# A selective scan with softplus of two pieces side by side, a diagonal product on TensorE and another order of products and scans

## The chip, the core and the metric

The kernel runs on one core of a Trainium2 chip. The metric is the device time of one execution in microseconds (us). Engines are named TensorE (PE in the profile; PEld is its weight load), VectorE (DVE), ScalarE (ACT), GpSimd (POOL) and SyncE (SP, which here only issues DMAs).

## The reference, cut to what matters

The reference has two layers on `x` of shape (8, 64, 64, 96): a convolution with a four-way selective scan, then attention without softmax and a quantized feed-forward part. Only the scan is touched by the change:

```python
# B = 8, L = 4096, D_INNER = 192, D_STATE = 16, DT_RANK = 6, K = 4 directions
x_dbl = jnp.einsum('bkdl,kcd->bkcl', xs, x_proj_weight)
dts, Bs, Cs = x_dbl[:, :, :6], x_dbl[:, :, 6:22], x_dbl[:, :, 22:]
dts = jnp.einsum('bkrl,kdr->bkdl', dts, dt_projs_weight)
delta = jax.nn.softplus(dts + dt_projs_bias[None, :, :, None])
A = -jnp.exp(A_logs).reshape(K, D_INNER, D_STATE)
def step(h, inps):                     # along L, one h for each channel and state
    d_t, u_t, b_t, c_t = inps
    h = h * jnp.exp(d_t[..., None] * A) + (d_t * u_t)[..., None] * b_t[:, :, None, :]
    y = jnp.einsum('bkdn,bkn->bkd', h, c_t)
    return (h, y)
# then y + D * u, and the sum over the four directions
```

## The kernel before, in words

`pass1` makes the normalized input, its projections, the convolution with SiLU (`u`), and the projections to dt, B and C, all to HBM scratch. `pass2` is the scan. `pass3` does everything from the layer norm on. The change lies in `pass2` and in the class `Slots`.

**Tiling of the scan.** `pass2` works on 192 pieces. A piece (index `at`) is 128 channel rows by T = 1024 positions. The 192 channels of a pair of batches are cut into three chunks: c = 0 and c = 1 are 128 channels of one batch each, c = 2 holds the remaining 64 channels of both batches (so a "half" in what follows is one batch's 64 rows of it). For each of 4 pairs, 3 chunks and 4 directions `k` there are 4 pieces in a row, with directions 2 and 3 running backwards. 128 pieces have c < 2, 64 have c = 2.

**What one piece does.** `prepare` loads `xdt` (the split parts of dt), `xb` (the parts of B) and `u`; TensorE makes `bT` (B with positions on partitions) and the product of `xdt` and `dt_w`; ScalarE makes `delta` from that by softplus; GpSimd makes `du` = delta * u; TensorE transposes it and ScalarE copies it out as `duT`. Then for each of 16 states n:

- `decay`: ScalarE makes `da` = exp(delta * A_n), in one of three buffers.
- the input of the scan, `dbu` = du * B_n in a PSUM buffer `wide` (three of them), in one of three ways. By ScalarE (`scaled`): eight multiplications of `duT` blocks with a column of `bT`, sixteen halves where c = 2, giving `x`, and eight transposes on TensorE. By GpSimd (`scaled_by_pool`): the same in one multiplication (two where c = 2), giving `xg`. Otherwise TensorE spreads B_n over the partitions with two bf16 matmuls, and VectorE multiplies that by `du` in place. `WAYS` lists, for c < 2 and for c = 2, the states of the first and of the second way; those left over take the third, which this document calls products on VectorE.
- `scan`: VectorE's tensor_tensor_scan of `da` and `dbu` into half of an `h` tile (two states in one, three tiles). `carries` has ScalarE copy the last column, for the next piece of the same direction.
- `times_c`: for every two states GpSimd multiplies `h` by C, loaded broadcast over partitions by SP (`load_c`, six buffers `c`).
- `sum_over_n`: TensorE transposes these products into the accumulator `acc` and so sums over n. For k = 0 the sum begins with `ud` = u times the sum of D over the directions, made by ScalarE and transposed; for k >= 2 it begins with the earlier direction's `ys`. `take_acc` copies `acc` to `y`.

**What sets the order.** Every engine is wrapped in `InOrder`: its instructions run in the order in which the program issues them. That order comes from `weave`, a planner that runs while the kernel is built. Each unit of work is a generator that yields (engine, cost in us, delay before its result is usable, optional buffer slots) or a key that it waits for. `weave` always takes the step that can begin first by its own clock and, among equals, that of lower rank. The rank is `at * N + n - lead`, and the lead is the number given in `add`. A second table says how many units of a kind can be open at once. `Slots` plans when a buffer comes free.

Of the kernel before, what the change touches and what calls it, by code (L numbers as in the profile page):

```python
# [54 lines left out]
WAYS = [([2, 5, 6, 8, 11, 12, 14, 15], [3, 7]), ([2, 3, 7, 9, 14], [0, 5, 12])]  # L55
NS = 3

# [70 lines left out]
class Slots:  # L128


    def __init__(self, count):
        self.count, self.taken, self.ends = count, 0, {}

    def when(self):

        return 0.0 if self.taken < self.count else self.ends.get(self.taken + 1 - self.count)
# [405 lines left out]
def pass2(ctx, tc, g, ident, engines, fixed, u_d, xd_d, b_d, dt_d, y_d):  # L542
# [7 lines left out]
    room = {"c": 6, "da": 3, "h": 3, "x": 3, "wide": 3, "xg": 1, "ud": 1, "acc": 1}  # L550
# [8 lines left out]
    done, counts, made, ys, carry = {}, {}, {}, {}, {}  # L559
# [13 lines left out]
    def prepare(at):  # L573
# [10 lines left out]
        yield "sp", 2.5, 3.0  # L584
        xdt = one.tile([2 * NS * NS * R, T], BF16, name="xdt")
        queue = sp if at else pool
        for j in range(2):
            for m in range(NS):
                row = (j * NS + m) * NS * R
                queue.dma_start(xdt[row : row + NS * R, :], dt_d[2 * pair + j][o][k2].rearrange("s r t -> (s r) t")[:, cols])  # L590
        if at > 0:
            yield "sp", 1.5, 3.0
# [18 lines left out]
        yield "pe", 0.9, 0.2, slots["wide"]  # L611
        pd, slot = take("wide", [P, T])
        for q in range(0, T, GRP):
            pe.matmul(pd[:, q : q + GRP], dt_w[:, c, k, :], xdt[:, q : q + GRP], start=True, stop=True)

        end = yield "act", 3.6, 0.2
        delta = two.tile([P, T], F32, name="delta")
        act.activation(delta, pd, AF.Softplus, bias=dt_b[:, c // 2, k : k + 1])
        slots["wide"].release(slot, end)
        made[at] = [xb, u, delta, None, None, bT]  # L620
        done["delta", at] = end
        end = yield "pool", 2.37, 0.2
        du = two.tile([P, T], F32, name="du")
        pool.tensor_mul(du, delta, u)
        made[at][3] = du
# [6 lines left out]
        made[at][4] = two.tile([P, NT, P], F32, name="duT")  # L632
        act.copy(made[at][4], pt)
        slots["wide"].release(slot, end)
        done["duT", at] = end

# [18 lines left out]
    def decay(at, n):  # L655

        _, c, k, _ = pieces[at]
        yield "delta", at
        end = yield "act", 1.06, 0.2, slots["da"]
        da, slot = take("da", [P, T])  # L660
        act.activation(da, made[at][2], AF.Exp, scale=a_neg[:, c // 2, k, n : n + 1])
        made["da", at, n] = da, slot
        done["da", at, n] = end

    def scaled(at, n):

        pair, c, _, _ = pieces[at]
        yield "duT", at
        x, (_, _, _, _, duT, bT) = None, made[at]
        for i in range(0, NT, 2):  # L670
            cost = 0.6 if c < 2 else 1.0
            end = yield ("act", cost, 0.2) if i else ("act", cost, 0.2, slots["x"])
            if i == 0:
                x, slot = take("x", [P, NT, P])
            for i2 in (i, i + 1):
                for j, (part, _, _) in enumerate(chunk_rows(pair, c)):
                    act.mul(x[:, i2, part], duT[:, i2, part], bT[:, i2, j * N + n : j * N + n + 1])
        made["x", at, n] = x, "x", slot
        done["x", at, n] = end

    def scaled_by_pool(at, n):
# [4 lines left out]
        _, _, _, _, duT, bT = made[at]  # L686
# [7 lines left out]
    def products(at, n):  # L694
# [3 lines left out]
        if n in by_act or n in by_pool:  # L698
            yield "x", at, n
            end = yield "pe", 1.3, 0.2, slots["wide"]  # L700
# [5 lines left out]
        else:  # L706
# [6 lines left out]
            end = yield "dve", 1.22, 0.0  # L713
            dve.tensor_mul(dbu, made[at][3], dbu)
# [3 lines left out]
    def scan(at, n):  # L718
# [6 lines left out]
        if n % 2 == 0:  # L725
            end = yield "dve", 2.26, 0.2, slots["h"]
            made["h", at, n // 2] = take("h", [P, 2, T])
            done["begun", at, n // 2] = 0.0
        else:
            yield "begun", at, n // 2  # L730
            end = yield "dve", 2.26, 0.2
# [39 lines left out]
    def sum_over_n(at, m):  # L771
# [10 lines left out]
        if m == 0 and k == 0:  # L782
            yield "delta", at
            yield "act", 1.05, 0.2, slots["ud"]
            ud, slot = take("ud", [P, T])
            act.mul(ud, made[at][1], dsum[:, c // 2 : c // 2 + 1])
            end = yield "pe", 1.2, 0.0, slots["acc"]
            made["acc"] = take("acc", [P, NT, P])
            add(ud, True, False)
            slots["ud"].release(slot, end)  # L790
# [10 lines left out]
        for i in range(2):  # L801
            if m == 0 and k == 1 and i == 0:
                end = yield "pe", 1.2, 0.0, slots["acc"]
                made["acc"] = take("acc", [P, NT, P])
            else:
                end = yield "pe", 1.2, 0.0
# [32 lines left out]
    for at, (pair, c, k, pc) in enumerate(pieces):  # L839
# [5 lines left out]
        add("prep", 8, prepare(at))  # L845
        for n in range(N):
            if n % 2 == 0:
                add("c", 12, load_c(at, n // 2), n)
            add("da", 2, decay(at, n), n)
# [6 lines left out]
            if n % 2 == 1:  # L856
                if at % NPC < NPC - 1:
                    add("carry", -2, carries(at, n // 2), n)
                add("term", 0, times_c(at, n // 2), n)
                add("sum", -4, sum_over_n(at, n // 2), n)  # L860
        add("acc", 0, take_acc(at), N)
    last = [(b, o, w) for b in range(LATE, NB) for o in range(2) for w in splits(b, o, b_d, dt_d)]
    units += [("split", 5 * N * (i + 1), late_split(*which)) for i, which in enumerate(last)]
    weave(units, {"prep": 1, "c": 1, "da": 2, "x": 1, "xg": 1, "dbu": 2, "scan": 2, "carry": 1, "term": 1, "sum": 1, "acc": 1, "split": 1}, done)
# [300 lines left out]
```

## Time and profile before

| What | Value |
| --- | --- |
| Time, median of 3 runs (lowest to highest) | 10121.8 us (10119.1 to 10127.6) |
| Span of the profiled execution | 10130.1 us |
| Scan pass in it: first scan begins, last ends | 719 us, 9328 us |
| Busy share of the span: VectorE, ScalarE, GpSimd, TensorE | 94%, 91%, 89%, 74% |
| Scans on VectorE with / without a carried value | 2304 of 2332 ns, 768 of 2271 ns |
| Products on VectorE (`wide<-du,wide`) | 1280 of 1208 ns |
| Exponentials on ScalarE (`da`) | 3072 of 1144 ns |
| `x` on ScalarE: whole blocks, halves | 8192 of 390 ns, 5120 of 335 ns |
| Table loads on ScalarE | 386 of 1283 ns |
| `c` times `h` on GpSimd | 1536 of 4557 ns |

The profile lists instructions by group: engine, operation, the tile written and the tiles read, count, busy time and mean duration, and after the bar the time in which the engine stood idle just before such an instruction, with what released it. Most instructions carry the line of the helper that records them (L91), so groups are told apart by tiles. Successive instructions of one engine overlap a little: the end of one lies behind the start of the next. What an instruction costs in a full queue is therefore its distance from start to start, which the timeline shows, and not its duration.

### The profile page before, as it was taken

How to read it: one execution, taken by the hardware profiler on the slowest of the kernel's cores; microseconds unless marked ns; L12 is line 12 of the kernel's file. 1: busy time of each engine (PE TensorE's matmuls, PEld its weight loads, DVE VectorE, ACT ScalarE, POOL GpSimd, SP SyncE). 2: the span in 40 equal slices, each digit the busy share in tenths (PEclk: the TensorE clock that was granted, in tenths of full speed). 3: DMA queues.
4: the chain of work that ended last, by engine and by line, in shares of the span. 5: the costliest groups of instructions: out<-in, count | busy, mean ns of one | idle time of the engine just before them, and what ended most of it. 6: DMA issues, size and time to landing. Idle time of an engine off the chain costs nothing.

```text
span 10130.1 us, 152413 instructions
## 1 busy us (share of the span) xinstructions
PE 7527.0 (74%) x52384; PEld 6235.5 (62%) x52384; DVE 9551.4 (94%) x7025; ACT 9186.9 (91%) x20692; POOL 8990.2 (89%) x2911
## 2 busy tenths in 40 slices
PE   7767777777777777777777777777777777776777
PEld 3336666665666666666666666655666666565666
DVE  7869999999999999999999999999999999998887
ACT  5669999999999999999999999999999999997776
POOL 1439999999999999999999999999999999998665
PEclk8889998989998989989999989999989999998887
DMA  5766776789976776799966766899767667998652
GB/s 167 233 205 215 225 236 217 229 210 206 209 219 213 225 218 214 223 211 200 223 211 214 230 212 223 212 205 209 217 213 225 218 212 224 208 203 183 192 151 77
DMA packets 932228, 2111.66 MB, mean 208 GB/s; under 512 B 274603, under 2 KB 422860, under 8 KB 929922
## 3 DMA queue, kind: packets, MB, share of 16 engines
q1 hardware_dynamic: 928650, 2100.57, 74.0%
q8 instruction: 419, 6.86, 0.3%
q14 instruction: 351, 2.88, 0.1%
q0 software_dynamic: 432, 0.94, 0.0%
q10 hardware_dynamic: 2376, 0.40, 0.0%
HBM read 1925.98 MB, written 175.66 MB: 207 GB/s over the span
## 4 chain that ended last, share of the span: by engine, by line
DVE 30%; ACT 29%; issue 15%; PE 13%; POOL 9%; DMA 3%; SPq 1%; DVEq 0%; ACTq 0%; POOLq 0%
DVE h L91 20%; ACT x L91 11%; ACT da L91 10%; POOL c L91 7%; PE acc L91 6%; DVE wide L91 5%; PE wide L91 3%; ACT L91 2%; ACT y L91 1%; POOL xg L91 1%; PE px L91 1%; PE pa L91 1%; ACT delta L91 1%; DMA xd_d<-xd 1%; DVE u L91 1%
## 5 line engine op out<-in xcount | busy, mean ns | idle before, releaser
L91 POOL TENSOR_TENSOR c<-c,h 128x2048 f32<-128x2048 f32 x1536 | 6959.5, 4557 | 300.0 <-issue 139.4
L91 DVE TENSOR_TENSOR_SCAN h<-da,carry,wide 128x1024 f32<-128x1024 f32 x2304 | 5268.3, 2332 | 137.5 <-PE wide L91 36.8
L91 ACT ACTIVATE x<-duT,bT 128x128 f32<-128x128 f32 (+1 forms) x13312 | 3970.8, 369 | 2.0
L91 PE MATMUL acc<-ident,c 128*128 128x128 f32 x24576 | 3439.1, 298 | 571.0 <-POOL c L91 563.3
L91 ACT ACTIVATE da<-delta,a_neg 128x1024 f32<-128x1024 f32 x3072 | 3513.4, 1144 | 316.2 <-DVE h L91 303.1
L91 PEld LDWEIGHTS acc<-ident,c 128*128 128x128 f32 x24576 | 3123.4, 155 | 1005.5 <-POOL c L91 891.2
L91 PE MATMUL wide<-ident,x 128*128 128x128 f32 x10752 | 1560.7, 291 | 645.3 <-DVE h L91 586.4
L91 PEld LDWEIGHTS wide<-ident,x 128*128 128x128 f32 x10752 | 1306.9, 150 | 841.5 <-ACT x L91 399.4
L91 DVE TENSOR_TENSOR_SCAN h<-da,wide 128x1024 f32<-128x1024 f32 x768 | 1712.9, 2271 | 46.2 <-PE wide L91 14.0
L91 DVE TENSOR_TENSOR wide<-du,wide 128x1024 f32<-128x1024 f32 x1280 | 1544.0, 1208 | 39.9 <-PE wide L91 39.6
L91 PE MATMUL wide<-xb,sel 96*128 96x512 bf16 x2560 | 820.5, 404 | 697.4 <-DVE h L91 686.4
L91 POOL TENSOR_TENSOR xg<-duT,bT 128x512 f32<-128x512 f32 (+1 forms) x640 | 894.5, 1414 | 28.3 <-PE wide L91 15.2
L91 PEld LDWEIGHTS <-sel 96*128 96x128 bf16 x2560 | 232.7, 102 | 878.1 <-DVE h L91 626.3
L91 PE MATMUL wide<-ident,xg 128*128 128x128 f32 x3584 | 483.8, 279 | 119.0 <-DVE h L91 116.4
L91 ACT ACT_TABLE_LOAD x386 | 495.2, 1283 | 26.3 <-DMA w_qT<-in_WqT_b 19.5
L91 PEld LDWEIGHTS wide<-ident,xg 128*128 128x128 f32 x3584 | 412.6, 144 | 148.9 <-issue 111.2
L91 POOL TENSOR_TENSOR du<-delta,u 128x1024 f32<-128x1024 f32 x192 | 457.5, 2383 | 7.5 <-ACT delta L91 7.5
L91 DVE SCALAR_TENSOR_TENSOR u<-xpad,conv_w,u 128x4096 f32<-128x4096 f32 x96 | 450.9, 4697 | 1.9
L91 PE MATMUL px<-u,w_xp 128*128 128x512 f32 x512 | 252.7, 633 | 63.4 <-ACT u L91 43.8
L91 POOL TENSOR_TENSOR gt<-gt,zs 128x512 f32<-128x512 f32 x128 | 161.8, 1275 | 132.1 <-ACT gt L91 111.9
L91 ACT COPY y<-acc 128x1024 f32<-128x1024 f32 x192 | 192.6, 1003 | 83.8 <-PE acc L91 83.5
L91 POOL TENSOR_TENSOR bq<-bq,bs 128x512 f32<-128x512 f32 (+1 forms) x48 | 115.1, 2400 | 166.9 <-ACT bs L91 155.1
(142 smaller groups left out, 5987.7 us busy)
## 6 DMA issues: line engine op xcount, KB each, us to landing
c<-xd_d SPq DMA_DIRECT2D x1024, 1024.0 KB
c<-xd_d SPq DMA_DIRECT2D x1024, 512.0 KB
u<-u_d SPq DMA_DIRECT2D x127, 512.0 KB
xdt<-dt_d SPq DMA_DIRECT2D x1146, 36.0 KB
xb<-b_d SPq DMA_DIRECT2D x382, 96.0 KB
u<-u_d SPq DMA_DIRECT2D x128, 256.0 KB
zs<-z_d SPq DMA_DIRECT2D x128, 256.0 KB
y_d<-y SPq DMA_DIRECT2D x24, 1024.0 KB
```

Source lines behind the costliest of these rows:

```text
L91: ins = getattr(self.engine, op)(*args, **kwargs).ins
```

## The change

Softplus is taken out of `prepare` into a new unit, `deltas_of`, which serves two successive pieces (SOFT = 2): it loads both `xdt`, multiplies each by `dt_w`, and runs both softplus with the planner's `da` slots held between them, so that no exponential is planned there. `delta` gets three buffers in place of two, `xdt` two in place of one. The start of the sum for k = 0 is no longer an `ud` made by ScalarE and eight transposes, but eight fp32 products of `u` with `d_diag`, a diagonal matrix of the summed D. The lists in `WAYS` are others; with c = 2 there are six states by ScalarE in place of five. In the planner some costs and leads are others, and a product on VectorE now has a delay of 0.22 before its scan.

```diff
-WAYS = [([2, 5, 6, 8, 11, 12, 14, 15], [3, 7]), ([2, 3, 7, 9, 14], [0, 5, 12])]
+WAYS = [([3, 5, 6, 10, 11, 12, 14, 15], [4, 13]), ([2, 6, 12, 13, 14, 15], [1, 3, 9])]
+SOFT = 2
...
     def when(self):
+        if self.held:
+            return None
...
+    three = ctx.enter_context(tc.tile_pool(name="p2three", bufs=SOFT + 1))
-    room = {"c": 6, "da": 3, "h": 3, "x": 3, "wide": 3, "xg": 1, "ud": 1, "acc": 1}
+    room = {"c": 6, "da": 3, "h": 3, "x": 3, "wide": 3, "xg": 1, "acc": 1}
...
+    d_diag = one.tile([P, 2, P], F32, name="d_diag")
+    for ty in range(2):
+        dve.tensor_scalar(d_diag[:, ty, :], ident, dsum[:, ty : ty + 1], None, ALU.mult)
...
     def prepare(at):
...
-        yield "sp", 2.5, 3.0
-        xdt = one.tile([2 * NS * NS * R, T], BF16, name="xdt")
...
-        yield "pe", 0.9, 0.2, slots["wide"]
-        pd, slot = take("wide", [P, T])
-        for q in range(0, T, GRP):
-            pe.matmul(pd[:, q : q + GRP], dt_w[:, c, k, :], xdt[:, q : q + GRP], start=True, stop=True)
-
-        end = yield "act", 3.6, 0.2
-        delta = two.tile([P, T], F32, name="delta")
-        act.activation(delta, pd, AF.Softplus, bias=dt_b[:, c // 2, k : k + 1])
-        slots["wide"].release(slot, end)
...
+        yield "delta", at
         end = yield "pool", 2.37, 0.2
         du = two.tile([P, T], F32, name="du")
-        pool.tensor_mul(du, delta, u)
+        pool.tensor_mul(du, deltas[at], u)
...
+    def deltas_of(first):
+
+        group = range(first, first + SOFT)
+        if first > 0:
+            yield "scans", first - 2
+        pds = []
+        for at in group:
...
+            yield "sp", 2.5, 3.0
+            xdt = two.tile([2 * NS * NS * R, T], BF16, name="xdt")
+            queue = sp if at else pool
...
+            pds.append(xdt)
+        for i, at in enumerate(group):
+            pair, c, k, pc = pieces[at]
+            yield "pe", 0.9, 0.2, slots["wide"]
+            pd, slot = take("wide", [P, T])
+            for q in range(0, T, GRP):
+                pe.matmul(pd[:, q : q + GRP], dt_w[:, c, k, :], pds[i][:, q : q + GRP], start=True, stop=True)
+            end = yield "act", 2.3, 0.2
+            slots["da"].held = i < SOFT - 1
+            deltas[at] = three.tile([P, T], F32, name="delta")
+            act.activation(deltas[at], pd, AF.Softplus, bias=dt_b[:, c // 2, k : k + 1])
+            slots["wide"].release(slot, end)
+            done["delta", at] = end
...
-            cost = 0.6 if c < 2 else 1.0
+            cost = (0.585, 0.965)[c // 2]
...
-            end = yield "pe", 1.3, 0.2, slots["wide"]
+            end = yield "pe", 1.0, 0.2, slots["wide"]
...
-            end = yield "dve", 1.22, 0.0
+            end = yield "dve", 1.22, 0.22
...
-            end = yield "dve", 2.26, 0.2, slots["h"]
+            end = yield "dve", 2.18 if first else 2.24, 0.2, slots["h"]
...
         if m == 0 and k == 0:
-            yield "delta", at
-            yield "act", 1.05, 0.2, slots["ud"]
-            ud, slot = take("ud", [P, T])
-            act.mul(ud, made[at][1], dsum[:, c // 2 : c // 2 + 1])
-            end = yield "pe", 1.2, 0.0, slots["acc"]
+            yield "u", at
+            yield "pe", 1.9, 0.0, slots["acc"]
             made["acc"] = take("acc", [P, NT, P])
-            add(ud, True, False)
-            slots["ud"].release(slot, end)
+            for i in range(NT):
+                pe.matmul(
+                    made["acc"][0][:, i, :], made[at][1][:, i * P : (i + 1) * P], d_diag[:, c // 2, :],
+                    start=i % (GRP // P) == 0, stop=False, skip_group_check=True,
+                )
...
-        add("prep", 8, prepare(at))
+        if at % SOFT == 0:
+            add("soft", 10, deltas_of(at))
+        add("prep", 12, prepare(at))
         for n in range(N):
             if n % 2 == 0:
-                add("c", 12, load_c(at, n // 2), n)
-            add("da", 2, decay(at, n), n)
+                add("c", 10, load_c(at, n // 2), n)
+            add("da", 1, decay(at, n), n)
...
                 if at % NPC < NPC - 1:
-                    add("carry", -2, carries(at, n // 2), n)
+                    add("carry", -4, carries(at, n // 2), n)
                 add("term", 0, times_c(at, n // 2), n)
-                add("sum", -4, sum_over_n(at, n // 2), n)
-        add("acc", 0, take_acc(at), N)
+                add("sum", -6, sum_over_n(at, n // 2), n)
+        add("acc", -2, take_acc(at), N)
```

## The prediction

> **What bounds the kernel now.** I read the busy shares first, then the time by stage, then the groups of instructions, then the waits, and last the timelines of single engines. The page's first line names no single limit:
>
> ```profile
> PE 7527.0 (74%) x52384; PEld 6235.5 (62%) x52384; DVE 9551.4 (94%) x7025; ACT 9186.9 (91%) x20692; POOL 8990.2 (89%) x2911
> ```
>
> Everything that the change touches lies in the scan pass, from 719 us (first scan) to 9328 us (end of the last): 8609 us for 192 pieces. The windows view of one pair of batches, 32 pieces with c < 2 in the first row and 16 with c = 2 in the second:
>
> ```profile
> 2884.00:4288.00 1404.00, 1075.41 (x7939) 921.98 (x7938) 1372.30 (x704) 1352.55 (x2945) 1350.15 (x354) 0.92 0.70 219
> 4288.00:5029.00 741.00, 537.08 (x3781) 453.24 (x3780) 725.90 (x385) 694.57 (x1740) 712.79 (x239) 0.90 0.93 208
> ```
>
> A piece takes 1404/32 = 43.9 us and 741/16 = 46.3 us here; over the whole pass, from first scan to first scan, 44.1 and 46.3 (128 x 44.1 + 64 x 46.3 = 8608). VectorE is at 98% in both rows, GpSimd and ScalarE at 94 to 96%. The groups of the scan pass:
>
> ```profile
> L91 POOL TENSOR_TENSOR c<-c,h 128x2048 f32<-128x2048 f32 x1535 | 6954.9, 4557 | 298.9 <-issue 138.3 <-DVE h L91 118.6 <-POOL du L91 20.2
> L91 DVE TENSOR_TENSOR_SCAN h<-da,carry,wide 128x1024 f32<-128x1024 f32 x2304 | 5268.3, 2332 | 137.5 <-PE wide L91 36.8 <-ACT x L91 5.3 <-DVE wide L91 1.5
> L91 ACT ACTIVATE da<-delta,a_neg 128x1024 f32<-128x1024 f32 x3069 | 3510.1, 1144 | 316.2 <-DVE h L91 303.1
> L91 DVE TENSOR_TENSOR wide<-du,wide 128x1024 f32<-128x1024 f32 x1278 | 1541.7, 1208 | 30.4 <-PE wide L91 30.1 <-issue 0.2
> L91 ACT ACT_TABLE_LOAD x382 | 490.1, 1283 | 6.8
> ```
>
> The last columns tell who waits: ScalarE's exponentials and GpSimd's products wait for VectorE (303 and 119 us, and the 138 us under "issue" fall largely where the scan they need was still running), VectorE waits for little. VectorE is the bound; the other two are close behind.
>
> Its timeline shows a loss that the idle column hides:
>
> ```profile
> 3010.82 1.20 DVE L91 TENSOR_TENSOR wide<-du,wide 128x1024 f32<-128x1024 f32 x1
> 3012.16 4.58 DVE L91 TENSOR_TENSOR_SCAN h<-da,carry,wide 128x1024 f32<-128x1024 f32 x2
> 3016.66 1.21 DVE L91 TENSOR_TENSOR wide<-du,wide 128x1024 f32<-128x1024 f32 x1
> 3017.97 4.58 DVE L91 TENSOR_TENSOR_SCAN h<-da,carry,wide 128x1024 f32<-128x1024 f32 x2
> 3022.47 1.21 DVE L91 TENSOR_TENSOR wide<-du,wide 128x1024 f32<-128x1024 f32 x1
> 3023.59 4.71 DVE L91 TENSOR_TENSOR_SCAN h<-da,carry,wide 128x1024 f32<-128x1024 f32 x2
> ```
>
> Read starts, not durations. A scan after a scan starts 2.24 us later (2.18 without a carry). After a product the next scan starts 1.31 to 1.34 us later in the first two cases and 1.12 in the third. Over the pass such distances fall into two heaps: some 1,045 at 1.31, some 207 at 1.12. I read the long ones as scans that take the product just written, the short ones as scans of another state. 1,045 x 0.195 = 204 us.
>
> ScalarE around one softplus:
>
> ```profile
> 3041.61 1.28 ACT L91 ACT_TABLE_LOAD   x1
> 3042.91 1.11 ACT L91 ACTIVATE delta<-wide,dt_b 128x1024 f32<-128x1024 f32 x1
> 3043.92 0.68 ACT L91 ACTIVATE x<-duT,bT 128x128 f32<-128x128 f32 x2
> 3044.62 1.28 ACT L91 ACT_TABLE_LOAD   x1
> 3045.92 1.15 ACT L91 ACTIVATE da<-delta,a_neg 128x1024 f32<-128x1024 f32 x1
> ```
>
> Each piece pays two table loads of 1.30 us from start to start, 1.01 us for softplus, and goes 3045.92 - 3041.61 = 4.3 us without beginning an exponential.
>
> **What the Trainium skill says.** "ScalarE: Activation LUTs", What ACT_TABLE_LOAD costs, gives some 1283 ns for the load and about 2.66 us with a drain behind it; the trace has the 1283 ns, but softplus starts 1.30 us after it, so I charge 1.30. The same page, Table sets: the hidden batching unit, says that cheap functions are in every set; the trace agrees (the scaled copies x run between softplus and the second load and cause none). "VectorE: DVE Perf Modes", The DRAIN you can't avoid, says that the flush comes after every operation and that a semaphore costs nothing extra; here the distance after a product is 1.12 or 1.31 us, so the measurement decides: which scan follows matters. "SBUF — State Buffer", SBUF: two separate sides, says that a VectorE operation with two SBUF inputs shuts out GpSimd; scans and products here have one input in PSUM, and scans keep their 2.24 us beside a busy GpSimd, so I expect no new contention.
>
> **The change part by part, in us per piece.** First each engine's work now, from start-to-start distances.
> - VectorE, c < 2: 12 x 2.24 + 4 x 2.18 + 6 x 1.12 = 42.3, and 5 of 6 products before their own scan, 1.0: 43.3. c = 2, with 8 products: 44.6 + 1.4 = 46.0. So it adds only 0.8 and 0.3 of other waiting.
> - GpSimd: 8 x 4.51 + 2.34 for du + 2 x 1.87 for xg = 42.2; for c = 2, six halves at 1.02: 44.5.
> - ScalarE, c < 2: 16 x 1.04 exponentials, 64 x 0.293 for x, 2.6 loads, 1.0 softplus, 0.9 + 0.9 copies of duT and y, 0.5 carries, 0.15 bT, 1.04/4 for ud: 41.7. c = 2: 80 halves of x at 0.239 and slightly dearer copies: 42.2.
>
> *Softplus in pairs.* 96 pairs need 192 loads instead of 384: -1.30 per piece on ScalarE. It isn't the bound, so alone this gives almost nothing; it makes room. On SP the same 1,152 xdt DMAs are issued, now twelve in a row (2.17 us for six in the trace, so 4.3). SP is in order; the xb, u and c loads queue behind them, but SP spends 5317 of the 7500 us from 1000 to 8500 us waiting for TensorE's sums to free a c buffer, and GpSimd hardly waits for c loads: 0. The held slot adds a wait: no exponential may come between the two softplus. Behind it stand the scans; the price is in the rivals.
>
> *u times D by TensorE.* 48 ud of 1.04 us leave ScalarE: -0.26 per piece. Eight fp32 products take the place of eight transposes; no row shows that form, the nearest is acc<-y,ident (16 in 2.05 us, about 1.0 for eight, as the transposes). Bounds: -0.1 to +0.9 us each, at most 43 us on an engine 26% idle; I take 0, hidden behind scans. Two d_diag instructions at the start: 0.
>
> *Other states.* c < 2 keeps 8 by ScalarE, 2 by GpSimd, 6 products on VectorE, differently placed. c = 2 gets a sixth by ScalarE: +16 x 0.24 = 3.8 there, one product fewer (-1.12) on VectorE, on TensorE eight transposes for two matmuls (+0.4, hidden).
>
> *Order.* The planner's 0.22 delay behind a product makes another ready scan come first; that takes off up to 1.0 (c < 2) and 1.4 (c = 2). dbu has two open units and wide three buffers, so this can be done most of the time. In exchange a wide buffer is held a scan longer: what is late next is TensorE's filling of wide, for which VectorE waits 81 us over the pass now. Bounds for that: 0 to as much again, 0.4 per piece.
>
> New floors: c < 2: VectorE 42.3, GpSimd 42.2, ScalarE 40.1. c = 2: VectorE 43.5, GpSimd 44.5, ScalarE 42.2 - 1.30 - 0.26 + 3.8 = 44.4. So the bound moves from VectorE to a tie. Two equal engines with three h buffers between them can't both be full; I allow 0.9 over the floor for c < 2 (0.5 to 1.6; 0.8 today with one bound) and 0.8 for c = 2 (0.3 to 1.8; three engines within 1 us). That gives 43.2 and 45.3: savings 0.9 x 128 = 115 and 1.0 x 64 = 64, 179 together. At the start the first exponential now waits for the second piece's xdt and softplus, some 3 us behind 712.5, partly covered by VectorE's first products: I charge 4. Sum: -175. Against the profiled span of 10130.1 this is 9955; the median of the runs, 10121.8, lies 8.3 below that span, so I forecast 9947.
>
> **Rivals.**
> *All waits shrink* (12%): the pieces follow GpSimd at 42.6 and 44.8. Savings 1.5 x 128 + 1.5 x 64 = 288: 9834. For it: VectorE idles only 2.5% now. Against: GpSimd has never been the bound here.
> *The order isn't what it says* (15%): the next scan mostly isn't ready, since its wide or da is missing, and products keep their 1.31. Then c < 2 gains nearly nothing and c = 2 one product: 64 x 1.3 = 84 less some 35 of jams on ScalarE: about 10075. For it: da holds three buffers and its lead is cut from 2 to 1.
> *The pair starves the scans* (13%, slower): between exponentials lie 1.30 + 1.01 + a gap + 1.01 + 1.30 = 4.6 us and the gap, in which the second product xdt x dt_w needs a wide buffer of its own: 0.7 to 2 us. With 1.04 for the next exponential, VectorE sees no new da for 6.4 to 7.7 us. Three filled da feed it 3 x 2.24 + products 1.3 = 8.0 us, two only 5.3. If ScalarE, lacking slack in c = 2, goes in with two, it loses up to 2.4 us per pair, 96 x 2.4 = 230 against the 175: +55, about 10177. The point of turning is 1.8 us lost per pair. Against: today's 4.3 us stretch makes VectorE wait for da by only some 3 us in all.
>
> **How the numbers follow.** The likeliest case has 58%, the three rivals 40%, 2% are left for no change. A difference of 0.2%, about 20 us, is what a measurement of this kernel can tell. Faster: 58 + 12 and most of the 15 = 82%; the same 5%; slower 13%. The range takes the likeliest case with the bounds of its allowances (9860 to 10060), the rival at 10075 with some 30 on top, and the upper part of the first rival: 9850 to 10105; outside are most of the slower case and half of the first rival.
>
> **What would show it.** Right: 192 fewer table loads; no ud; 1,216 products on VectorE, most followed by a scan at 1.12; pieces at about 43.2 and 45.3; GpSimd's idle before c falling below 200 us; ScalarE at some 98% in the c = 2 windows. Wrong: products still at 1.31; VectorE idle before scans released by da in blocks of over 1.8 us near each pair; pieces of c = 2 above 46.

## The result, and the profile after

| Kernel | Median | Ratio to before, with its 95% interval |
| --- | --- | --- |
| before (12 runs) | 10115.8 us | 1 |
| changed (12 runs) | 10111.0 us (10100.5 to 10122.6) | 0.9995 [0.9987, 1.0003] |

The change makes no difference that can be measured. The forecast was 9947 us, with 5% for "the same", and the result lies just above its range. In what follows, the distance of a kernel from the changed one is the difference of the two ratios to before, times 10116 us.

Yet most of the work that was to go is gone. The first line of the page of the changed kernel, and four of its groups (busy us, mean ns; behind the bar, idle us just before and what ended it):

```profile
PE 7534.7 (74%) x53152; PEld 6321.7 (62%) x53152; DVE 9414.7 (93%) x6963; ACT 9110.8 (90%) x21476; POOL 9004.2 (89%) x2911
...
L92 POOL TENSOR_TENSOR c<-c,h 128x2048 f32<-128x2048 f32 x1536 | 6960.2, 4557 | 245.5 <-DVE h L92 207.3
L92 DVE TENSOR_TENSOR_SCAN h<-da,carry,wide 128x1024 f32<-128x1024 f32 x2304 | 5241.1, 2327 | 143.8 <-PE wide L92 78.0
...
L92 ACT ACTIVATE da<-delta,a_neg 128x1024 f32<-128x1024 f32 x3072 | 3507.0, 1144 | 178.5 <-DVE h L92 164.0
...
L92 DVE TENSOR_TENSOR wide<-du,wide 128x1024 f32<-128x1024 f32 x1216 | 1446.9, 1209 | 144.3 <-PE wide L92 115.6
```

VectorE is 137 us less busy and waits more: 115.6 us before products for TensorE's `wide`, where the kernel before had 30.1. ScalarE does less too; its wait for VectorE fell by half. The groups of the scan pass alone have half the table loads:

```profile
L92 ACT ACT_TABLE_LOAD x191 | 245.1, 1283 | 3.4
```

The stages (same columns as before; here for a whole pair: 32 pieces with c < 2, then 16 with c = 2):

```profile
2898.00:4294.00 1396.00, 1057.81 (x8001) 923.95 (x7999) 1362.97 (x706) 1314.44 (x2928) 1356.59 (x360) 0.93 0.70 222
4294.00:5041.00 747.00, 545.06 (x3908) 468.06 (x3909) 702.90 (x370) 718.85 (x1963) 713.83 (x240) 0.90 0.93 207
```

The c = 2 row shows what happened: VectorE's busy time fell from 725.9 to 702.9 us, but the stage takes 747 us in place of 741. Over the pass a piece takes 43.66 us for c < 2 (44.08 before) and 46.79 us for c = 2 (46.33 before).

Since durations overlap, I made VectorE's account from its starts: each distance to the next start, less 2.24 us for a scan with a carry, 2.18 without, 1.12 for a product. An excess of 0.15 to 0.26 us behind a product I count as a scan that takes that product (a dependent pair), a larger one as a wait. (On this count the kernel before waits 104 us; the 137 us that some expectations name is the page's idle time before its scans.)

| Us over the scan pass | before | changed | difference |
| --- | --- | --- | --- |
| Products (1278, 1214 seen) | 1431 | 1360 | -71 |
| Dependent pairs (1038, 265) | 213.5 | 53.8 | -160 |
| Waits | 103.6 | 315.5 | +212 |
| Small remainder | | | -6 |
| First scan to last scan | 8606.3 | 8581.1 | -25 |
| First scan begins | 718.9 | 739.4 | +20.5 |

So 231 us of VectorE's work left, 212 us came back as waits and 20 us at the start. The lines of the waits view for VectorE (us, times, longest us) say for whom; first the kernel before, then the changed one:

```profile
DVE h L91 <- PE wide L91: 50.8, 51, 3.8
DVE wide L91 <- PE wide L91: 30.1, 31, 1.1
```

```profile
DVE h L92 <- PE wide L92: 125.0, 123, 5.6
DVE wide L92 <- PE wide L92: 115.6, 64, 6.7
...
DVE h L92 <- ACT da L92: 27.4, 36, 2.5
```

Waits for TensorE's filling of `wide` went from 81 to 241 us, with single ones of 5.6 and 6.7 us. They are uneven: by place in a direction the four pieces with c = 2 take 45.23, 50.35, 44.94 and 46.64 us (before: 45.96, 46.39, 46.47, 46.51). Something delays the second piece of each four. TensorE's own waits name one cause; the kernel before has no such line:

```profile
PE wide L92 <- DMA xb<-b_d: 102.0, 33, 9.5
```

One such place in the changed kernel, all engines in the order of time (SPq is SP's queue; start and duration in us; in brackets the idle time before and its releaser):

```profile
4326.18 11.32 SPq L92 DMA_DIRECT2D c<-xd_d  x8
4337.54 1.05 SPq L92 DMA_DIRECT2D xb<-b_d  x2
...
4343.01 0.60 PE L92 MATMUL wide<-xb,sel 96*128 96x512 bf16 x2
...
4347.04 1.20 DVE L92 TENSOR_TENSOR wide<-du,wide 128x1024 f32<-128x1024 f32 x1
...
4351.28 0.38 PE L92 MATMUL wide<-sel,xb 96*128 96x32 bf16 x8 [7.68 <-DMA xb<-b_d]
...
4352.55 1.23 DVE L92 TENSOR_TENSOR wide<-du,wide 128x1024 f32<-128x1024 f32 x1 [4.31 <-PE wide L92]
```

`xb` is issued at 4337.54, behind eight `c` loads, and TensorE can begin with it 13.7 us later. In the trace the `bT` made from it begins 8.5 to 11.0 us after the issue (medians by place with c = 2; 14.2 to 15.0 in the kernel before). So TensorE, which runs in order, stands 7.68 us before it with the next spreads of B behind, and VectorE runs dry for 4.31 us. The DMA engines are full at that time:

```profile
4338.00:4344.00 6.00, 4.77 (x34) 3.70 (x34) 6.00 (x4) 6.00 (x20) 6.00 (x4) 1.00 1.04 223
```

The column before the last is the DMA share, 1.04. The load can't simply be issued sooner: `xb` has two buffers, and `prepare` waits for the scans of piece at - 2. Measured back from the first scan of its piece, TensorE comes to `bT` 9 to 11 us earlier than before where c < 2 and 9 to 17 us earlier where c = 2, while the issue of `xb` moved by 3 to 10 us (medians by place). The lead of `prepare` (8 became 12) can have moved `bT`, and so can the loads of `xdt`, which no longer stand ahead of it in `prepare`; no run separates the two.

The start is lost at SP too. Its queue, TensorE and VectorE at the first scan of the changed kernel:

```profile
708.96 4.39 SPq L92 DMA_DIRECT2D c<-xd_d  x5
...
713.40 12.33 SPq L92 DMA_DIRECT2D xdt<-dt_d  x6
...
733.49 1.01 PE L92 MATMUL wide<-xdt,dt_w 108*128 108x512 bf16 x2 [19.88 <-DMA xdt<-dt_d]
...
739.42 4.45 DVE L92 TENSOR_TENSOR_SCAN h<-da,wide 128x1024 f32<-128x1024 f32 x2
```

`deltas_of` sends the first piece's `xdt` through GpSimd's queue and the second's through SP, where it stands behind `c` loads; the held slot keeps every exponential until the second softplus has run.

### The profile page after: what moved, and what is told of

The parts are those of the page before. It is cut to its first block, busy times and chain, and to the rows that moved or that the text cites. A ratio compares the mean times of both kernels' runs of the same rounds, so it can differ in the third digit from the quotient of the medians.

```text
span 10120.1 us, 154630 instructions
## 1 busy us (share of the span) xinstructions
PE 7534.7 (74%) x53152; PEld 6321.7 (62%) x53152; DVE 9414.7 (93%) x6963; ACT 9110.8 (90%) x21476; POOL 9004.2 (89%) x2911
## 4 chain that ended last, share of the span: by engine, by line
ACT 29%; DVE 21%; PE 16%; issue 15%; POOL 13%; DMA 5%; SPq 1%; POOLq 0%; DVEq 0%; ACTq 0%
DVE h L92 15%; ACT x L92 12%; ACT da L92 11%; POOL c L92 9%; PE acc L92 7%; PE wide L92 5%; DVE wide L92 2%; ACT L92 2%; DMA xb<-b_d 2%; ACT delta L92 1%; POOL xg L92 1%; PE px L92 1%; DMA xd_d<-xd 1%; PE pa L92 1%; ACT y L92 1%
## 5 line engine op out<-in xcount | busy, mean ns | idle before, releaser
L92 POOL TENSOR_TENSOR c<-c,h 128x2048 f32<-128x2048 f32 x1536 | 6960.2, 4557 | 245.5 <-DVE h L92 207.3
L92 ACT ACTIVATE x<-duT,bT 128x128 f32<-128x128 f32 (+1 forms) x14336 | 4223.6, 367 | 77.8 <-PE wide L92 76.6
L92 PEld LDWEIGHTS acc<-ident,c 128*128 128x128 f32 x24576 | 3060.7, 152 | 941.0 <-POOL c L92 787.5
L92 PEld LDWEIGHTS wide<-ident,x 128*128 128x128 f32 x11264 | 1337.0, 148 | 685.7 <-DVE h L92 264.2
L92 DVE TENSOR_TENSOR wide<-du,wide 128x1024 f32<-128x1024 f32 x1216 | 1446.9, 1209 | 144.3 <-PE wide L92 115.6
L92 PE MATMUL wide<-xb,sel 96*128 96x512 bf16 x2432 | 759.6, 398 | 367.4 <-DVE h L92 350.8
L92 PE MATMUL wide<-ident,xg 128*128 128x128 f32 x3584 | 542.0, 301 | 183.5 <-DVE h L92 170.8
L92 PEld LDWEIGHTS wide<-ident,xg 128*128 128x128 f32 x3584 | 461.0, 157 | 229.2 <-issue 164.2
L92 PE MATMUL wide<-ident,du 128*128 128x128 f32 x1536 | 221.6, 291 | 229.7 <-DVE h L92 213.5
L92 PEld LDWEIGHTS wide<-ident,du 128*128 128x128 f32 x1536 | 181.7, 149 | 270.5 <-issue 204.4
```

Of the source, the lines that this page charges most:

```text
L92: ins = getattr(self.engine, op)(*args, **kwargs).ins
```

## The experiments

The theories go by letters in the expectations: A, loads that land too late for the plan (`xb` above all); B, ScalarE as the bound where c = 2; C, the changed leads; D, setting a product apart from its scan, which holds `wide` longer; E, TensorE costs in the planner that are too low; F, nothing but another order, of which the planner finds a better or worse one by chance. Except where it is said, edits are to the changed kernel, and an edit of a cost or a wait makes `weave` write a whole new order.

### Single suspects undone

**e1_start**: the second `xdt` through GpSimd's queue as well. The order of the compute engines stays.

```diff
-            queue = sp if at else pool
+            queue = sp if at >= SOFT else pool
```

> The changed kernel, but the xdt loads of both of the first two pieces go through GpSimd's queue and not SyncE's. Theory A (late loads took the gain back): the first scan, at 739 us in the changed kernel and 719 us before, comes back to 718 to 722 us, and the whole is 16 to 20 us shorter, about 10093 us. Rival B (ScalarE and GpSimd are the bound after the change) and rival C (the new leads of the planner jam the order) say the same of the start, but nothing else moves: pieces with c = 2 stay at 46.8 us. If the span shortens by less than 8 us, the start was made up for later.

Measured: 10105.4 us, 0.9985 [0.9979, 0.9992]; 10 us below the changed kernel. The first scan begins at 726.9 instead of 739.4:

```profile
720.97 1.01 PE L92 MATMUL wide<-xdt,dt_w 108*128 108x512 bf16 x2 [7.37 <-DMA xdt<-dt_d]
```

So the queue of that load is a cause of the late start: 12.5 of the 20.5 us are undone. TensorE still waits 7.37 us for the load.

**e2_landing**: tell the planner that `xb` and `u`, and `xdt`, land later, so that it puts their uses later.

```diff
-        yield "sp", 1.5, 3.0
+        yield "sp", 1.5, 12.0
...
-            yield "sp", 2.5, 3.0
+            yield "sp", 2.5, 12.0
```

> The changed kernel, but the planner is told that xb, u and xdt land 12 us after their issue in place of 3 us, so it places what needs them later. Theory A: TensorE's waits for the DMA of xb (102 us in the changed kernel) fall below 20 us, the second piece of each direction with c = 2 falls from 50.4 to about 46 us, VectorE's waits for wide from 241 to some 150 us, and the whole is 60 to 110 us shorter. Rival B: c = 2 stays above 46.5 us, since the engines have no more room; under 20 us. Rival C: under 30 us, the waits at states 4 and 5 of pieces with c < 2 stay.

Measured: 10219.7 us, 1.0098 [1.0081, 1.0115], 104 us above the changed kernel: a miss. The waits for `xb` vanish and the second piece with c = 2 falls from 50.4 to 47.5 us. But the plan now places softplus so late that VectorE stands for `da`, and for `du`, which GpSimd makes from the `delta` of softplus:

```profile
DVE h L92 <- ACT da L92: 122.2, 45, 4.3
DVE h L92 <- POOL du L92: 120.3, 47, 2.6
```

Here a late load was not mended by planning its use later, since everything of the next piece hangs on it.

**e3_ways**: the states for c = 2 as before (five by ScalarE, eight products).

```diff
-WAYS = [([3, 5, 6, 10, 11, 12, 14, 15], [4, 13]), ([2, 6, 12, 13, 14, 15], [1, 3, 9])]
+WAYS = [([3, 5, 6, 10, 11, 12, 14, 15], [4, 13]), ([2, 3, 7, 9, 14], [0, 5, 12])]
```

> The changed kernel with the states of before for c = 2 (five by ScalarE, eight products on VectorE). Theory A: ScalarE was not the limit; the floor of VectorE rises from 43.4 to 44.6 us, and pieces with c = 2 stay between 46 and 47.5 us, with the second of each direction still the longest; the whole is the same or up to 40 us longer. Rival B: with 3.8 us less on ScalarE per piece, c = 2 falls to about 45.3 us, 90 us less in all. Rival C: within 20 us.

Measured: 10173.0 us, 1.0054 [1.0039, 1.0069]: slower by 60 us (A said at most 40), with c = 2 at 47.6 us (46.79). B falls: five states on ScalarE don't help. The edit changes which states they are as well as their number, so it doesn't tell which of the two is worth the 60 us.

**e4_leads**: four leads as before.

```diff
-            add("da", 1, decay(at, n), n)
+            add("da", 2, decay(at, n), n)
...
-                    add("carry", -4, carries(at, n // 2), n)
+                    add("carry", -2, carries(at, n // 2), n)
...
-                add("sum", -6, sum_over_n(at, n // 2), n)
-        add("acc", -2, take_acc(at), N)
+                add("sum", -4, sum_over_n(at, n // 2), n)
+        add("acc", 0, take_acc(at), N)
```

> The changed kernel with the leads of before for the exponentials (2), the carries (-2), the sums (-4) and the copy of acc (0); the leads of prepare (12) and of the c loads (10) stay as changed. Theory A: xb is still late, TensorE's waits for it stay near 100 us, and the whole moves by under 25 us. Rival B: under 25 us. Rival C: VectorE's waits over 0.26 us fall from 315 towards the 137 us of before, and the whole is 80 to 150 us shorter.

Measured: 10171.9 us, 1.0054 [1.0039, 1.0069], 60 us above the changed kernel, which none of the three had expected; waits 358 us. C falls for these four together; the lead of `prepare` is not among them.

**g5_noapart** and **g7_pecost**: no delay behind a product; TensorE's costs as before.

```diff
# g5_noapart
-            end = yield "dve", 1.22, 0.22
+            end = yield "dve", 1.22, 0.0
# g7_pecost
-            end = yield "pe", 1.0, 0.2, slots["wide"]
+            end = yield "pe", 1.3, 0.2, slots["wide"]
...
-                end = yield "pe", 1.1, 0.0
+                end = yield "pe", 1.2, 0.0
```

> The changed kernel with the planner's delay behind a product at 0.0 as before, so that a product's own scan follows it again. Theory A: VectorE loses some 0.195 us on most of 1,216 products again and its waits stay at 315 us: 100 to 150 us longer, about 10240 us. Theory D: about 1,000 dependent pairs return, but VectorE's waits over 0.26 us fall from 315 to under 200 us, and the whole stays within 40 us of the changed kernel.

> The changed kernel with the planner's TensorE costs of before: 1.3 for eight transposes into wide and 1.2 for a sum, in place of 1.0 and 1.1. Theory E (with a mean granted clock of 0.905 the new costs are too low, so the order jams where the clock is halved): VectorE's waits for wide fall from 241 to under 150 us and the whole is 60 us or more shorter. Theories A and D: within 40 us of the changed kernel.

Measured: g5_noapart 10187.5 us, 1.0071 [1.0055, 1.0088]; 589 dependent pairs, not some 1000, and waits of 310 us, about as in the changed kernel (315). Without the delay the kernel is 77 us slower, so here setting apart pays and D falls for the changed kernel. The time lies between the numbers of A and D. g7_pecost 10115.8 us, 1.0002 [0.9993, 1.001], 7 us above the changed kernel: E falls.

**g6_apart**: the delay alone, put into the kernel before.

```diff
-            end = yield "dve", 1.22, 0.0
+            end = yield "dve", 1.22, 0.22
```

> The kernel before with one number changed: the planner's delay behind a product is 0.22 in place of 0.0. Theory A: the dependent pairs fall from 1,045 to under 350 and VectorE's waits stay near 137 us, since xb keeps its early place: 100 to 140 us shorter, about 10000 us. Theory D: the pairs fall as well, but the waits rise by as much, and the whole stays within 40 us of the kernel before.

Measured: 10219.5 us, 1.0106 [1.0091, 1.0121], 107 us slower than the kernel before. It does what the prediction's "Order" step wanted: dependent pairs 1038 to 499, 109 us gained. But waits go from 104 to 311 us, and 255 of these are for `wide` (134.0 + 120.6; 81 before):

```profile
DVE wide L91 <- PE wide L91: 134.0, 183, 1.3
DVE h L91 <- PE wide L91: 120.6, 89, 3.3
```

Neither A nor D had expected the kernel to get slower. These are many short waits and no late load. One of them, all engines in the order of time:

```profile
3049.38 2.35 DVE L91 TENSOR_TENSOR_SCAN h<-da,carry,wide 128x1024 f32<-128x1024 f32 x1
...
3051.79 1.03 PE L91 MATMUL wide<-xb,sel 96*128 96x512 bf16 x2 [2.99 <-DVE h L91]
...
3052.86 1.23 DVE L91 TENSOR_TENSOR wide<-du,wide 128x1024 f32<-128x1024 f32 x1 [1.13 <-PE wide L91]
```

TensorE waits until the scan frees a `wide`, then spreads B, and VectorE's next product waits for that: D's reason, at work in this kernel. Setting apart by itself, on the old lists, gives back twice what it takes. With the new lists (g5_noapart) it is worth 77 us. What an edit is worth depends on what else is in the plan.

### The late xb

**g1_xb**: `xb` loaded in `deltas_of`, beside `xdt`, a piece or more ahead, with three buffers; the planner knows.

```diff
-        yield "sp", 1.5, 3.0
+        yield "xb", at
+        yield "sp", 0.5, 3.0
...
-        xb = two.tile([KB, T], BF16, name="xb")
...
+        xb = xbs[at]
...
-            yield "sp", 2.5, 3.0
+            end = yield "sp", 3.5, 3.0
+            done["xb", at] = end
+            xbs[at] = three.tile([KB, T], BF16, name="xb")
...
```

> The changed kernel, but xb is loaded together with the paired xdt, a piece or more earlier, into three buffers; prepare then loads only u. Theory A (late xb blocks TensorE's queue): TensorE's waits for the DMA of xb, 102 us in the changed kernel, fall under 10 us, the second piece of each direction with c = 2 falls from 50.4 to 46 or 47 us, and the whole is 60 to 100 us shorter than the changed kernel, about 10030 us. Theory D (a product set apart from its scan holds its wide buffer a scan longer, so TensorE fills the next one late): under 30 us; the waits come back at other states.

Measured: 9994.3 us, 0.9884 [0.9869, 0.9898], 112 us below the changed kernel. VectorE's waits fall from 315 to 179 us and TensorE's for `xb` to

```profile
PE wide L92 <- DMA xb<-b_d: 17.9, 10, 3.3
```

But this edit also made a new order. Two kernels separate the two.

**h1_xbonly** and **i1_xball**: loads moved without a word to the planner, so that the order on every compute engine is that of the changed kernel. In h1_xbonly the odd pieces' `xb` goes with `xdt`; in i1_xball each piece's `xb` is loaded at least a piece ahead, in four buffers.

```diff
# load_xb (not shown) is the tile and the two loads that stood in prepare
# h1_xbonly, in prepare, and then in deltas_of after its xdt loads
+        if at % SOFT == 0:
+            load_xb(at, queue)
...
+            if at % SOFT:
+                load_xb(at, queue)
...
# i1_xball, at the same two places
+        if at == 0:
+            load_xb(at, queue)
...
+            if at + 1 < len(pieces):
+                load_xb(at + 1, sp)
```

> The changed kernel with one thing moved: xb of the second piece of each pair is issued right behind the pair's xdt, a piece earlier, into three buffers. The planner's steps are untouched, so TensorE, VectorE, ScalarE and GpSimd run the same instructions in the same order; only SyncE's queue differs. Theory A (the late xb blocks TensorE): TensorE's waits for xb fall from 102 us to 40 or less, the second piece of each direction with c = 2 from 50.4 to under 47.5 us, and the whole is 60 to 110 us shorter. Theory F (the earlier-xb kernel gained because the planner came to another order): within 20 us of the changed kernel.

> The changed kernel with every xb issued at least a piece earlier, into four buffers, and the order of TensorE, VectorE, ScalarE and GpSimd unchanged. The piece in which TensorE was blocked, the second of each direction with c = 2, is the one in which bT of the third, an even piece, is made; moving the odd ones could not help it. Theory A: TensorE's waits for xb fall below 15 us, that piece from 50.4 to about 46 us, the whole 60 to 100 us shorter, near 10030 us. Theory F (the planner's order is the cause): the waits for xb vanish, but others take their place, and the whole moves by under 25 us.

Measured: h1_xbonly 10103.4 us, 0.9984 [0.9977, 0.9991], 11 us gained; TensorE still waits 51.1 us for `xb` and the second piece stays at 50.5 us. The trace shows why: what is late during the second piece is the `xb` of the third, an even one (counted from 0), and I had moved the odd ones. i1_xball moves all: 10067.9 us, 0.9955 [0.994, 0.997], 40 us below the changed kernel. No wait for `xb` is left on TensorE, the second piece takes 48.67 us, VectorE's waits fall by 55 us to 261:

```profile
DVE h L92 <- PE wide L92: 110.3, 115, 2.9
DVE wide L92 <- PE wide L92: 73.9, 51, 9.7
```

This lies between A's and F's numbers. With the order held still, the late `xb` costs 40 us, give or take some 15 by the intervals; 4.5 of them lie at the start, where the first scan begins at 734.9 us. The other 70 us or so of g1_xb are a difference: they came with the new order, and no run takes them apart further. The second piece is mended only in part: at 48.67 us it is still 3.6 us longer than the mean of the other three (4.7 us in the changed kernel).

### How much an order varies by itself

**i2_replan**, **i3_replan2** (in the changed kernel), **j1_before_replan**, **j2_before_replan2** (in the kernel before): a planner's cost moved by 0.005 or 0.05, which is meant to say nothing but makes a new order.

```diff
# i2_replan
-            cost = (0.585, 0.965)[c // 2]
+            cost = (0.59, 0.97)[c // 2]
# i3_replan2
-            end = yield "pe", 1.0, 0.2, slots["wide"]
+            end = yield "pe", 1.05, 0.2, slots["wide"]
# j1_before_replan
-            cost = 0.6 if c < 2 else 1.0
+            cost = 0.605 if c < 2 else 1.005
# j2_before_replan2
-            end = yield "pe", 1.3, 0.2, slots["wide"]
+            end = yield "pe", 1.35, 0.2, slots["wide"]
```

> The changed kernel, with the planner's cost of the multiplications on ScalarE at 0.59 and 0.97 in place of 0.585 and 0.965: the same instructions in another order. Theory A: within 25 us of the changed kernel, since xb stays as late. Theory F: 30 us or more away, up or down; the change's leads and costs are then one draw among orders that differ by as much as the change could bring.

> The changed kernel, with the planner's cost of eight transposes into wide at 1.05 in place of 1.0: another order of the same work. Theory A: within 25 us of the changed kernel. Theory F: 30 us or more away, up or down.

> The kernel before with the planner's cost of the multiplications on ScalarE at 0.605 and 1.005 in place of 0.6 and 1.0: the same work in another order. If the order of before was a favourable draw, 30 us or more longer; if not, within 25 us.

> The kernel before with the planner's cost of eight transposes into wide at 1.35 in place of 1.3. If the order of before was a favourable draw, 30 us or more longer; if not, within 25 us.

Measured: i2_replan 10138.7 us, 1.0023 [1.0011, 1.0034]; i3_replan2 10100.3 us, 0.9981 [0.9974, 0.9988]; j1_before_replan 10140.0 us, 1.0021 [1.0014, 1.0027]; j2_before_replan2 10119.3 us, 1.0001 [0.9992, 1.001]. So against their own base +28, -14, +21 and +1 us. In these four draws the order alone moves the time by up to some 30 us. The two re-plans of the kernel before don't show it to be an uncommonly good draw that ate the gain, and I read nothing from differences under 30 us between two orders. Three orders of the kernel before (1, 1.0021, 1.0001) and three of the changed one (0.9995, 1.0023, 0.9981) lie over each other, and none comes near the forecast, so the missing gain is not one bad order either.

### Together

**h2_best**: g1_xb and e1_start. **h3_ud**: h2_best with `ud` by ScalarE and eight transposes as before. **h4_nohold**: h2_best without the held slots (the line below is taken out). **i4_replan_best**: h2_best with the meaningless cost of i2_replan.

```diff
# h3_ud
-            yield "u", at
-            yield "pe", 1.9, 0.0, slots["acc"]
+            yield "delta", at
+            yield "act", 1.05, 0.2, slots["ud"]
+            ud, slot = take("ud", [P, T])
+            act.mul(ud, made[at][1], dsum[:, c // 2 : c // 2 + 1])
+            end = yield "pe", 1.2, 0.0, slots["acc"]
...
# h4_nohold
-            slots["da"].held = i < SOFT - 1
# i4_replan_best
-            cost = (0.585, 0.965)[c // 2]
+            cost = (0.59, 0.97)[c // 2]
```

> The kernel with xb in the paired load, and xdt and xb of the first two pieces through GpSimd's queue. Theory A: first scan 5 to 14 us earlier than its 733 us, about 9984 us in all, the shortest of the kernels so far. Theory F says the same; if the start does not move, SyncE's queue was not what held it.

> The kernel with early xb and early start, but u times D made by ScalarE and transposed, as before the change. If ScalarE's 48 instructions of 1.04 us were on the path, it is 30 to 50 us longer; if they lay beside other work (the prediction's view: they make room only), within 20 us, up or down by what another planner's order brings.

> The kernel with early xb and early start, but without holding the exponentials back between the two softplus, so most pairs pay four table loads. Theory A and the prediction: ScalarE has 1.3 us per piece less room, pieces with c = 2 (ScalarE's floor 44.4 us becomes 45.7 us) grow by about 1 us, c < 2 hardly; 40 to 90 us longer. Rival (the hold starves VectorE, as the prediction's slower case had it): VectorE's waits for da, 25 us with the hold, vanish and the kernel is 20 us or more shorter.

> The kernel with early xb and early start, with the planner's cost of the multiplications on ScalarE at 0.59 and 0.97. Theory A: the gain of early xb holds in another order, 9960 to 10020 us. Theory F: the 9986 us was a lucky order; 10030 us or more.

Measured: h2_best **9985.7 us, 0.9872 [0.9857, 0.9887]**, the fastest kernel of the study. Its first scan begins at 714.7 us, VectorE waits 196 us, a piece takes 43.31 us for c < 2 and 45.76 for c = 2. Its stages:

```profile
2850.00:4241.00 1391.00, 1056.99 (x8006) 915.98 (x8006) 1363.25 (x705) 1315.43 (x2931) 1362.04 (x366) 0.94 0.72 224
4241.00:4971.00 730.00, 545.77 (x3900) 466.86 (x3901) 701.11 (x369) 716.45 (x1965) 714.15 (x240) 0.90 0.95 212
```

The same busy times on VectorE, ScalarE and GpSimd as in the changed kernel to within 2.5 us in the second row, and 17 us less time: what went is waiting.

i4_replan_best, 10010.6 us, 0.9895 [0.988, 0.9909]: another order, 23 us slower, and most of the gain is still there, so it doesn't hang on one order. h3_ud, 10014.5 us, 0.9898 [0.9883, 0.9912]: 26 us slower, within what an order does, so the diagonal product is worth between nothing and some 50 us.

h4_nohold, 10235.8 us, 1.0119 [1.0103, 1.0134]: 250 us above h2_best, where I had expected far less. Without the held slots exponentials slip in between the two softplus, and the table loads are back (h2_best has 190 in its scan pass):

```profile
L92 ACT ACT_TABLE_LOAD x381 | 488.8, 1283 | 6.6
```

and VectorE's waits, of which those two lines had 89.7 and 27.4 us in h2_best:

```profile
DVE h L92 <- PE wide L92: 221.6, 182, 3.5
DVE h L92 <- ACT da L92: 91.1, 73, 3.1
```

The extra 190 loads take 245 us of ScalarE; VectorE's waits grow by 241 us (196 to 437), far more than the 30 us of the re-plans. That a microsecond of ScalarE costs about a microsecond of time, though ScalarE has the smaller busy share, would fit, but is not shown: the planner goes on charging 2.3 us for a softplus, the price with shared loads (3.6 in the kernel before), so the plan is also out of step with ScalarE here, and no run separates the two.

## Why the prediction was wrong

**The work was right.** A scan that takes the product just before it costs 0.2 us more, and all counts came: 192 fewer table loads, no `ud`, 1,216 products, dependent pairs down by 160 us. No kernel's mean piece went below the new floors. Of the signs for "wrong" one came true, pieces with c = 2 above 46 us; of those for "right" two did not: GpSimd's idle time before `c` is 245.5 us and not below 200, and ScalarE is busy for 96% of the c = 2 stage and not 98%.

**The bound was right only as busy time.** VectorE was the busiest engine, but the chain of work that ended last (the page follows it back from the end, in shares of the whole span; before, then changed) ran over all engines already:

```profile
DVE 30%; ACT 29%; issue 15%; PE 13%; POOL 9%; DMA 3%; SPq 1%; DVEq 0%; ACTq 0%; POOLq 0%
ACT 29%; DVE 21%; PE 16%; issue 15%; POOL 13%; DMA 5%; SPq 1%; POOLq 0%; DVEq 0%; ACTq 0%
```

VectorE's part went down by 9 points and those of TensorE, GpSimd and the DMAs up, which a sum of each engine's work with one allowance for waiting can't see.

**Step that failed first: "the xb, u and c loads queue behind them ... : 0".** It looked at SP's free time and at GpSimd's waits for `c`, not at how long a small load takes to land and what on TensorE stands behind its first use. And the lead of `prepare`, in the diff, was given no price. Measured: 102 us of waiting on TensorE, 40 us of time (i1_xball, the order unchanged).

**"Bounds for that: 0 to as much again, 0.4 per piece", for the filling of `wide`.** It was (241 - 81)/192 = 0.83 per piece, twice the upper bound. The prediction gave one reason, a `wide` held a scan longer, and its sum has no term for TensorE's other stops. In g6_apart, on the old lists, the named reason is most of it: 109 us of dependent pairs gained, 207 us of waits come for it. In the changed kernel it is small. For each of VectorE's waits for `wide` I went back in the trace to TensorE's last stop of over 0.1 us, as far as 2.5 us before the wait began:

| Us of VectorE's waits for `wide`, by TensorE's last stop | before | g6_apart | changed | i1_xball |
| --- | --- | --- | --- | --- |
| For a scan to free a `wide`, for a spread of B or transposes | 32 | 132 | 12 | 10 |
| The same, for a product of `xdt` | 0 | 5 | 26 | 26 |
| For a load of `xb` or `xdt` | 0 | 0 | 59 | 22 |
| For ScalarE's copy of `acc` | 0 | 0 | 53 | 50 |
| For GpSimd's product of `c` and `h` | 24 | 73 | 9 | 8 |
| Others | 1 | 2 | 7 | 2 |
| No such stop | 24 | 42 | 75 | 67 |
| All | 81 | 255 | 241 | 184 |

This names what came last, not what a mend would gain, and with a reach of 5 us the rows shift: `acc` has 63 us in the changed kernel and 31 have no stop. But 138 of the 241 us stand behind late loads, the copy of `acc` and the products of `xdt`, behind which nothing stood before; the reason that was priced has 12 us, less than before, or 38 with the products of `xdt`.

**"I charge 4" at the start.** It was 20.5 us. The step took some 3 us for the second `xdt` and softplus; that `xdt` is issued through the other queue behind five `c` loads and takes 20 us from the first issue to its product. e1_start gives back 10 us of time.

**The diagonal product.** "About 1.0 for eight" was mis-sized: the eight show as sixteen matmuls, 768 in all for 48, and take 2.05 us. The sixteen of acc<-y,ident were eight products too, so the line was misread. Against 1.04 us for the eight transposes of `ud` at their shortest in the kernel before, that is 1.0 us more, a little above the stated bound of 0.9. No time lost to it is shown (h3_ud).

**The rivals.** "The pair starves the scans" had the right outcome (the gain eaten) for a reason that the trace refutes: VectorE's waits for `da` are 27.4 us over the pass, of at most 2.5 us, 0.3 us per pair and not 2.4. Nor did taking the hold away help (h4_nohold, 250 us worse). "The order isn't what it says" is refuted by 265 dependent pairs. "All waits shrink" is what h2_best goes towards (43.3 and 45.8 us), without reaching it.

**What stays open.** The late `xb` (40 us) and the first `xdt` (10 us of the 20 at the start) are shown with the order unchanged. Together that is some 50 of the 164 us between the forecast and the result; h2_best gets some 125 us, and the rest of that came with the new order. Of the 196 us of waits left in it, and of the 261 in i1_xball, I have no experiment that splits them. The table above gives candidates: `acc`, which has one buffer, with spreads of B behind its copy to `y` (TensorE's waits for that copy, before and changed):

```profile
PE acc L91 <- ACT y L91: 31.4, 67, 1.5
PE acc L92 <- ACT y L92: 99.0, 98, 2.3
```

then the pair's two products of `xdt`, which wait for a free `wide` and hold it until softplus, and their loads: in the second piece with c = 2 of i1_xball, late `xdt` stand behind 18 of VectorE's 67 us of waits. The lead of `prepare` on its own is a rival as well. None of these was tried.

## What to carry to other kernels

Where a planner writes the order, look at whether loads land when the plan thinks they do: compare, in the trace, each small load's distance from issue to first use with its distance from issue to landing in the busiest DMA stretch. If it is short, load earlier with one more buffer; telling the planner to use it later cost 104 us here, the earlier load with a new plan gained 112. Before crediting a lead, a list or a cost with a gain, re-plan the unchanged kernel with a cost altered by a hair: here that alone moved the time by up to 30 us. And before pricing a wait by one reason, list every stop of the engine that is waited for: here TensorE, 26% idle, stood for loads and for `acc` just when the next `wide` was due.

## What the runs showed of the hardware

A small load behind large ones took long here: `xb`, behind eight `c` loads, took 13.7 us from issue to first use, with TensorE idle for it, at a DMA share of 1.04. Issuing took longer as well: six `xdt` issues took 12.33 us at the start behind five `c` loads, against 2.17 us in the prediction's count (the median over the pass; 3.5 us in the changed kernel). What in the queue or the DMA engines makes it so is not shown.

A dependency on the instruction just before costs VectorE some 0.2 us: a scan begins 1.31 us after the product that it takes, as the distances are read here, and 1.11 to 1.12 us after another. In the changed kernel's timeline most products have the short distance, as here:

```profile
5521.83 1.21 DVE L92 TENSOR_TENSOR wide<-du,wide 128x1024 f32<-128x1024 f32 x1
5522.94 2.33 DVE L92 TENSOR_TENSOR_SCAN h<-da,carry,wide 128x1024 f32<-128x1024 f32 x1
```
